# Memory sets between layer 1's gathers, its rows zero-filled in two halves within the layer, and some of layer 0's routing asked for later

## The chip, the cores and the metric

The kernel runs on one core of a Trainium2 chip. The core has a tensor engine (TensorE, PE in the profile) with its weight loads (PEld), a vector engine (VectorE, DVE), a scalar engine (ScalarE, ACT), GpSimd (POOL), and SyncE (SP), which here only issues DMAs. The metric is device time in microseconds (us) of one execution; the number that counts is the median of several.

## What is computed

Two transformer layers in float32, over 8 batches of 256 tokens with 128 channels. Each layer is an attention and a mixture of experts (MoE), each behind a layer norm whose scale and shift come from a conditioning vector. In short:

```
h = layernorm(x) * (1 + ca) + sa
x = x + ga * attention0(h)        # causal, 16 heads of 8, with biases
h = layernorm(x) * (1 + cb) + sb
x = x + gb * ffn0(h)              # shared gelu expert 128-512-128
                                  # + the best 2 of 8 such experts, softmax gates
h = layernorm(x) * (1 + ca) + sa
x = x + ga * attention1(h)        # causal, 16 heads of 64, no biases
h = layernorm(x) * (1 + cb) + sb
x = x + gb * ffn1(h)              # h + shared SwiGLU expert 128-64-128
                                  # + the best 2 of 16 such experts, sigmoid gates
```

The modulation vectors `sa` to `gb` are different for the two layers.

## The kernel before

**Stages.** The order of all instructions on each engine is the order in which the Python program asks for them; there is no scheduler. Layer 0's attention is a loop of 24 units, three for a batch, and layer 1's one of 32 units, four for a batch. A unit asks for its scores (PE), their exponentials (ACT, L1136 and L1673), the causal selects (POOL, L822) and, in the next unit, the product with the values (`o`, L1154 and L1692). Other work is hung on the units by number: `at(n, ...)` asks for it ahead of a unit's values, `at_end(n, ...)` behind everything of that unit, and `at_head(n, head, ...)` behind the causal select of one of its heads.

**Routing.** Tokens are sorted to experts in DRAM. For a span of batches the router's logits give each token's two best experts (a dozen small DVE operations, L850 to L857), PE counts how many earlier tokens chose the same expert (`rk`, L917 to L920), DVE turns that into a row number (`at`, `pick`, `slot`, `idx`, L922 to L928), and POOL writes the tokens to their rows by indirect DMAs, called scatters (L932). Each of these pieces is one step of a generator, so that they can be asked for apart: a step is one `go()`. The rows of layer 0 are `xs` of object `z0` (8.4 MB), those of layer 1 `xs` of object `z1` (24,576 rows of 128 floats, 12.6 MB). Both are zeroed first, since rows that no token takes are read too: `clear` (L888) issues one DMA on SP's queue that writes a zero tile over and over. Both fills are issued in set-up, one behind the other, and the loads of layer 0's expert weights (`wst`, L1495) come after them on the same queue. The first scatter of each layer waits for its fill.

**Layer 0's MoE** runs all its tokens in 39 tiles of 128 rows through the experts, beside the start of layer 1. The gates of its shared path: `gates0` (L1249 on) takes the difference of the two best logits on DVE, a tanh on ACT (L1252), and two more operations on DVE; `turn_gates0(w)` (L1284 on) transposes them on PE (`gp`, L1285) and copies them to SBUF (`gT`, L1288), on ACT for the first two windows of 512 tokens. Layer 0's routing hangs on the units in spans of batches (0,1), (2,3), (4), (5), with the first two spans' ranks asked for with `at(n + 4, go)`.

**Layer 1's MoE.** Batches 0 to 5 are sorted, scattered and run in 10 groups of 4 tiles (`turn1`, `hidden1`, `project_tiles`), and POOL fetches the results back for each token with 24 indirect DMAs, called gathers: `gather1(j)` for j = 0 to 11, two each (L1058). Batches 6 and 7 are not sorted: they go through all 16 experts, weighted by the gates: `dense_hidden(p)` for p = 0 to 7 computes two experts' gate and up products on PE (`gud`, L1942), a SiLU on ACT and a product on DVE (`a`, L1936 and L1937); `dense_gate` multiplies by the gates (L1947) and `dense_project` projects (`of`, L1952). `combine1` adds the gathered rows, weighted, on PE (`of`, L2018).

**The end of the program.** Behind the last group's projection the program asks for the 24 gathers; then for gates, `weigh1` (the diagonal matrices `dg`, L2010, on ACT), the shared expert and `dense_hidden(0)`; `gate_rows(1)` (the transpose `gT`, L1917, copied by DVE in L1919); `dense_hidden(1)` and `(2)`; the second step of `flag()`; `dense_hidden(3)`, and so on to `dense_hidden(7)` with combines and projections between. The products `gud`, `gT` and `good_cnt` share one PSUM tag of two buffers, taken in turn, so each waits until the one before the last has been read. `flag()` sets `bad`, which decides whether a general fallback has to run; it does not in the runs here:

```
yield
cnt = pp.tile([1, 1], F32, tag="s", name="good_cnt")
nc.tensor.matmul(out=cnt, lhsT=whole, rhs=nums[:, 1:2], start=True, stop=True)
nc.vector.tensor_scalar(bad, cnt, most[0:1, :], 1.0, ALU.is_lt, ALU.mult)
```

`most` is a tile of one column that holds a constant. Layer 0 has a helper that writes this constant again with POOL, `apart_on_gpsimd()` (L1404 and L1405), and `scatter(go, times)` calls it ahead of each of layer 0's scatters.

**The last batch of layer 1's attention** is normalised by `spread_last(us)` for two units at a time: PE spreads the reciprocals (`rp`, L1733) and DVE multiplies (L1737); `finish1(B - 1)` then projects it (`y`, L1745).

Of the kernel before, what the change touches and what calls it, by code (L numbers as in the profile page):

```python
# [9 lines left out]
F32 = mybir.dt.float32  # L10
# [6 lines left out]
P = 128  # L17
# [15 lines left out]
WAIT = mybir.DependencyInfo(mybir.DependencyClass.Sync, mybir.DependencyReason.DATA)  # L33
# [524 lines left out]
def fast_path(ctx: ExitStack, tc: tile.TileContext, i: dict, out: bass.AP, bad: bass.AP):  # L558
# [3 lines left out]
    nc = tc.nc  # L562
# [60 lines left out]
    for base, cm, step in ((0, 1, -D0), (D0 - 1, -1, D0)):  # L623
        nc.gpsimd.affine_select(
            out=hm, in_=hm, compare_op=ALU.is_ge, fill=0.0, base=base,
# [93 lines left out]
    def spread(t, rd, first, n):  # L719

        nc.sync.dma_start(
            out=t.rearrange("p k b c -> p (k b c)"),
            in_=rd[first : first + n].rearrange("k b c -> (k b c)").partition_broadcast(P),
        )
# [136 lines left out]
    class Sorted:  # L861


        def __init__(self, pool, tag, ne, nt, nd):
            self.pool, self.tag, self.ne, self.nt, self.nd = pool, tag, ne, nt, nd
            self.cap = cap = nt * P
            self.placed = 0
            f32 = lambda shape, name: pool.tile(shape, F32, name=f"{name}{tag}")
            self.s12 = f32([P, nt, 2, ne], "s12")
            self.slot = f32([P, nt, 2], "slot")  # L870
            self.region = f32([P, ne], "region")

            self.seen = pool.tile([P, nt + 1, ne], BF16, name=f"seen{tag}")
            self.yidx = pool.tile([P, nt, 2], I32, name=f"yidx{tag}")
            self.rowi = pool.tile([P, nd], I32, name=f"rowi{tag}")
            self.widx = pool.tile([P, nd], I32, name=f"widx{tag}")
            self.xs = dram.tile([ne * cap, P], F32, name=f"xs{tag}")
            self.ys = dram.tile([(ne + nd) * P, P], F32, name=f"ys{tag}")
            nc.gpsimd.tensor_scalar(self.region, num[:, :ne], float(cap), 0.0, ALU.mult, ALU.add)
            nc.gpsimd.memset(self.seen[:, 0, :], 0.0)  # L880
            self.marks = [pool.tile([P, 7, ne], BF16, name=f"marks{tag}{n}") for n in range(E1 // ne)]
            for t in self.marks:
                nc.gpsimd.memset(t[:, 0:3, :], 0.0)
# [1 line left out]
        def tmp(self, shape, name, dt=F32, bufs=2):  # L885
            return self.pool.tile(shape, dt, tag=name, bufs=bufs, name=f"{name}{self.tag}_{self.n}")

        def clear(self, zero):  # L888
            m = zero.shape[1]
            self.fill = nc.sync.dma_start(  # L890
                out=self.xs.rearrange("(p a) c -> p (a c)", p=P).rearrange("p (n m) -> p n m", m=m),
                in_=zero.unsqueeze(1).to_broadcast([P, self.ne * self.cap // m, m]),
            ).ins
            self.scatters = []

        def place(self, *args):
            for _ in self.place_steps(*args):
# [39 lines left out]
        def apart(self, ins):  # L937


            group = f"scatters{self.tag}"  # L940
            if self.scatters:
                tc.declare_no_dep(ins, group=group, reason="different rows")
                tc.add_manual_dep(ins, self.fill.name, WAIT, reason="rows are cleared first")
            tc.add_to_no_dep_group(group, ins)
            self.scatters.append(ins)

# [105 lines left out]
                in_offset=bass.IndirectOffsetOnAxis(ap=self.widx[:, d : d + 1], axis=0),  # L1052
            )

        def gather(self, yg, j):

            for k in range(2):
                nc.gpsimd.indirect_dma_start(  # L1058
                    out=yg[:, k, :], out_offset=None, in_=self.ys[:, :],
                    in_offset=bass.IndirectOffsetOnAxis(ap=self.yidx[:, j, k : k + 1], axis=0),  # L1060
                )
# [13 lines left out]
    SPANS0 = ((0, 2), (2, 2), (4, 1), (5, 1), (6, 1), (7, 1))  # L1075
# [169 lines left out]
    def gates0(first, nt):  # L1245

        ts = bass.ds(first, nt)
        g = g12[:, ts]
        name = f"g0_{first}"  # L1249
        th = ap0.tile([P, nt, 1], F32, tag="red", name=f"th{name}")  # L1250
        nc.vector.tensor_tensor(th, g[:, :, 0:1], g[:, :, 1:2], ALU.subtract)
        nc.scalar.activation(th, th, AF.Tanh, scale=0.5)  # L1252
        yield
        nc.vector.tensor_scalar(g[:, :, 0:1], th, 0.5, 0.5, ALU.mult, ALU.add)
        nc.vector.tensor_scalar(g[:, :, 1:2], th, -0.5, 0.5, ALU.mult, ALU.add)
        pick = ap0.tile([P, nt, 2, E0], F32, tag="pickg", bufs=1, name=f"pick{name}")
        nc.vector.tensor_tensor(pick, z0.s12[:, ts], g.unsqueeze(3).to_broadcast([P, nt, 2, E0]), ALU.mult)
        nc.vector.tensor_tensor(gates[:, ts, 0:E0], pick[:, :, 0, :], pick[:, :, 1, :], ALU.add)
# [24 lines left out]
    def turn_gates0(w):  # L1283
        gp = ps_ln([P, P], f"gp0_{w}")  # L1284
        nc.tensor.transpose(gp, gates[:, bass.ts(w, TT), :].rearrange("p j e -> p (j e)"), ident)  # L1285
        gT = hid0["g", w] = ap0.tile([P, P], F32, tag="gT", bufs=2, name=f"gT0_{w}")
        if w < 2:
            nc.scalar.copy(gT, gp)  # L1288
        else:
            nc.vector.tensor_copy(gT, gp)  # L1290

    def shared_project0(w):
        for _ in shared_project_steps0(w):
# [97 lines left out]
    def at(n, *steps):  # L1391
        early.setdefault(n, []).extend(steps)

    def at_end(n, *steps):
        ends.setdefault(n, []).extend(steps)
# [28 lines left out]
    for w in range(1, NW):  # L1424
        measure, normalise, modulate = layernorm_parts(w, md[0], SA, CA, f"0a{w}", ps_ln)
        n = 6 * w - 6
# [6 lines left out]
    ways = {}  # L1433
# [9 lines left out]
    for bs in SPANS0[:4]:  # L1443
        n = 3 * sum(bs) + 2
        measure, normalise, modulate, tokens = norms0[bs]
        go = ways[bs] = one(route0(bs))
        at_end(n, measure)
        at(n + 2, modulate)
        if bs[1] > 1:
            at(n + 2, tokens)  # L1450
        at_end(n + 2, go)
        if bs[1] == 1:
            at_end(n + 2, tokens)
        if bs[0] < 5:
            at(n + 3, go)
        if bs[0] < 4:
            at(n + 4, go)
        elif bs[0] == 4:
            at_end(n + 4, go)
        for unit, head in spots[bs[0]]:  # L1460
            at_head(unit, head, lambda go=go: scatter(go, 1))
    first_gates, last_gates = one(gates0(0, 8)), one(gates0(8, 8))
    at_end(17, first_gates)
    at_end(20, first_gates)
    norm6, norm7 = norm0(SPANS0[4]), norm0(SPANS0[5])
    at_end(23, norm6[0], lambda: turn_gates0(0), lambda: turn_gates0(1), lambda: ways[SPANS0[3]]())

    project0(0)
    project_v0(0)
# [3 lines left out]
    zero = ap0.tile([P, 512], F32, tag="hst", bufs=3, name="zero")  # L1473
# [8 lines left out]
    def set_up():  # L1482
        rd0 = rows_of(0, md[0])
        spread(mdb0, rd0, GA, 4)
        spread(gb0.unsqueeze(1), rd0, GB, 1)
        w1.update({n: load(w1p, n, nc.sync) for n in ("wo1", "gate_w", "wg1", "wu1", "wd1")})
        for n in range(2):
            nc.sync.dma_start(out=wds1[bass.ts(n, I1), :], in_=i["wds1"])
        nc.sync.dma_start(out=gate_b, in_=i["gate_b"].partition_broadcast(P))
        nc.sync.dma_start(out=bp32, in_=i["bp32"])  # L1490
        z0.clear(zero)
        z1.clear(zero)
        for e in range(E0 - 3):
            wst.append(ap0.tile([P, WPK], F32, tag=f"wst{e}", bufs=1, name=f"wst{e}"))
            nc.sync.dma_start(out=wst[e], in_=i["wpk"][bass.ts(e, P), :])  # L1495
        nc.gpsimd.memset(gates, 0.0)
        nc.gpsimd.memset(gates[:, :, E0 : E0 + 1], 1.0)
# [56 lines left out]
    scatter(go7, 4)  # L1554
    hides[1]()
    hides[1]()
    last_gates()
    one(shared_add0(0))()
    hides[1]()
# [437 lines left out]
    sums, diags = {}, {}  # L1997

    def gather1(j):
        k, n = divmod(j, 3)  # L2000
        if n == 0:
            sums["yg", k] = lp.tile([P, 3, 2, P], F32, tag="pt", bufs=4, name=f"yg1_{k}")
        z1.gather(sums["yg", k][:, n], j)

    def weigh1(w):

# [30 lines left out]
        return layernorm_parts(w, md[1], SA, CA, f"1a{w}", ps_ln)  # L2037

    spread(mdb1, rd1[0], GB, 4)
    nc.vector.memset(on, 0.0)  # L2040
    for n in range(4):
        nc.vector.memset(on[:, n, bass.ts(n, 8)], 1.0)
# [56 lines left out]
    for n in range(N):  # L2099
        b, u = divmod(n, 4)  # L2100
        scores1(b, u, behind.pop(n, {}))
        if n == 0:
            nc.gpsimd.memset(sel, 0.0)
            nc.gpsimd.affine_select(
                out=sel, in_=sel, compare_op=ALU.not_equal, fill=1.0, base=0,
                pattern=[[-8, 4], [-32, 2], [-64, 2], [0, D1]], channel_multiplier=1,
            )
        if n + 2 < N:
            project_qk1(*divmod(n + 2, 4))
        for step in early.pop(n, ()):  # L2110
            step()
        if n:
            values1(*divmod(n - 1, 4))
        if n + 2 < N:
            project_v1(*divmod(n + 2, 4))
        if u == 0 and b:
            reciprocals1(b - 1)
        for step in ends.pop(n, ()):
            step()

# [21 lines left out]
    norms[0][0]()  # L2142
    project_tiles(2)
    hidden1(4)
    spread_last((0, 1))
    turn1(5)
    norms[0][1]()
    project_tiles(3)
    norms[0][2]()
    spread_last((2, 3))  # L2150
    turn1(6)
    project_tiles(4)
    hidden1(5)
    go6()
    finish1(B - 1)
# [173 lines left out]
```

## Time and profile before

| | us |
|---|---|
| median of 14 runs | 604.07 |
| fastest and slowest of them | 598.14, 608.71 |
| the profiled execution | 607.14 |
| its span | 605.3 |

| engine | busy us | share of the span |
|---|---|---|
| PE | 542.7 | 90% |
| PEld (weight loads, beside PE) | 385.4 | 64% |
| DVE | 322.4 | 53% |
| POOL | 270.6 | 45% |
| ACT | 263.3 | 43% |

The page gives busy time per engine, then the span in 40 slices of about 15.1 us (a digit is the busy share in tenths, and in the row PEclk the clock that the throttle granted PE), the DMA queues, the chain of work that ended last, and the costliest groups of instructions. In a timeline line the numbers are start and duration; the brackets hold the idle time of the engine before the instruction and what ended it; "remote" there is a releaser that the profile doesn't show, "issue" is time in which the engine waited for nothing that it shows. The mean granted clock of the profiled execution was 0.959 of full speed. The 24 gathers of layer 1's end belong to the group of 56 at L1058, mean 962 ns each; the memory sets of layer 0 (L1405, 128x1) are 32, mean 112 ns. The fills move 20.5 MB of the 85.4 MB that all DMAs move.

### The profile page before, as it was taken

The numbers are of one execution on the slowest core, as the hardware profiler recorded it, in microseconds if no ns is written. First come the engines' busy times: TensorE is split into PE (matmuls) and PEld (weight loads), VectorE is DVE, ScalarE is ACT, GpSimd is POOL, SyncE is SP. The second block draws the span as 40 slices with busy tenths as digits, with TensorE's granted clock in tenths as the row PEclk, the third lists the DMA queues.
The fourth block names the chain that finished last, engine by engine and source line by source line (L and its number), as shares of the span: only waits on it lengthen the run. The fifth ranks groups of instructions, "written<-read, shape, count | busy, mean of one in ns | idle before, by whom it ended". The sixth has DMA issues, their size and how long they took to land.

```text
span 605.3 us, 11998 instructions
## 1 busy us (share of the span) xinstructions
PE 542.7 (90%) x4499; PEld 385.4 (64%) x4499; DVE 322.4 (53%) x986; ACT 263.3 (43%) x494; POOL 270.6 (45%) x400
## 2 busy tenths in 40 slices
PE   5999988899999998999999999999989898960594
PEld 4355544467999996666767676767667576830264
DVE  5258784675422224654456646556474957660154
ACT  3678764344566632763344423452625421250010
POOL 5224575664444214756223545340654530787300
PEclk9999997899999999999999999999999998996688
DMA  8699994234999813104030312103030366551401
GB/s 272 243 400 406 395 352 183 66 106 127 313 344 347 281 36 129 63 22 93 5 71 11 69 34 73 30 3 71 19 87 15 85 196 171 158 138 54 98 19 56
DMA packets 53566, 85.40 MB, mean 141 GB/s; under 512 B 6652, under 2 KB 32764, under 8 KB 52348
## 3 DMA queue, kind: packets, MB, share of 16 engines
q1 hardware_dynamic: 45308, 60.50, 31.5%
q0 software_dynamic: 8048, 23.67, 11.9%
q8 instruction: 37, 0.61, 0.4%
q10 hardware_dynamic: 144, 0.39, 0.2%
q14 instruction: 29, 0.24, 0.1%
HBM read 53.46 MB, written 31.07 MB: 140 GB/s over the span
## 4 chain that ended last, share of the span: by engine, by line
PE 74%; DVE 12%; another core or an unknown queue 6%; ACT 4%; issue 2%; DMA 1%; POOL 0%; DVEq 0%; ACTq 0%; POOLq 0%
PE sc L1670 7%; PE o L1692 6%; PE hp L1353 6%; PE yt L1361 6%; PE qp L1639 5%; PE y L1745 5%; PE sc L1120 5%; PE vp L1652 4%; PE kp L1639 4%; PE sum L1700 3%; PE o L1154 3%; PE gud L1942 2%; PE hp L1273 2%; PE qk L1084 2%; PE ysh L1302 2%
## 5 line engine op out<-in xcount | busy, mean ns | idle before, releaser
L822 POOL TENSOR_SCALAR_AFFINE_SELECT pt<-pt 128x256 f32<-128x256 f32 (+1 forms) x144 | 68.1, 500 | 154.2 <-ACT pt L1673 115.6
L1058 POOL DMA_INDIRECT yg<-ys,yidx x56 | 53.9, 962 | 38.3 <-DMA ys<-ysb 19.9
L1673 ACT ACTIVATE pt<-sc 128x768 f32<-128x768 f32 x64 | 48.4, 808 | 26.1 <-PE sc L1670 26.0
L1136 ACT ACTIVATE pt<-sc 128x1024 f32<-128x1024 f32 x48 | 46.6, 1027 | 20.1 <-PE sc L1120 15.5
L1670 PEld LDWEIGHTS sc<-q,k 64*128 64x128 f32 x512 | 41.5, 187 | 18.9 <-issue 13.9
L1670 PE MATMUL sc<-q,k 64*128 64x256 f32 (+1 forms) x512 | 50.5, 336 | 0.0
L1692 PE MATMUL o<-pt,v 128*64 128x256 f32 (+1 forms) x512 | 49.0, 332 | 1.7 <-DVE ou L1704 1.7
L1355 ACT ACTIVATE hst<-hp,wt 128x128 f32<-128x128 f32 x136 | 38.9, 369 | 25.7 <-ACT hst L1355 24.6
L1655 ACT COPY v<-vp 128x512 f32<-128x512 f32 x32 | 18.8, 586 | 67.1 <-PE vp L1652 67.1
L1050 POOL DMA_INDIRECT wt<-in_wpk_dram,widx x31 | 29.6, 953 | 33.9 <-PE xT L1344 29.8
L1692 PEld LDWEIGHTS o<-pt,v 128*64 128x64 f32 x512 | 32.0, 136 | 18.9 <-POOL pt L822 5.7
L1643 DVE COPY q<-qp 128x512 f32<-128x512 f32 x32 | 22.0, 688 | 35.9 <-PE qp L1639 35.9
L1639 PE MATMUL qp<-h,wq 128*128 128x256 f32 x128 | 36.1, 404 | 3.3 <-DVE q L1643 2.0
L1366 DVE COPY ysb<-yt 128x128 f32<-128x128 f32 x39 | 11.4, 292 | 50.0 <-PE yt L1361 50.0
L1120 PE MATMUL sc<-qm,k 32*128 32x512 f32 x192 | 35.8, 723 | 2.3 <-ACT pt L1136 1.7
L932 POOL DMA_INDIRECT xs<-ht0b,idx x32 | 32.1, 1002 | 12.0 <-issue 11.4
L1652 PE MATMUL vp<-wv,h 128*128 128x512 f32 x64 | 36.0, 645 | 0.0
L1353 PE MATMUL hp<-xTs,wt 128*128 128x128 f32 x272 | 35.9, 275 | 0.0
L1361 PE MATMUL yt<-wt,hst 128*128 128x128 f32 x272 | 35.8, 275 | 0.0
L1353 PEld LDWEIGHTS hp<-xTs,wt 128*128 128x128 f32 x272 | 33.0, 192 | 0.0
L1361 PEld LDWEIGHTS yt<-wt,hst 128*128 128x128 f32 x272 | 33.0, 192 | 0.0
L1639 PE MATMUL kp<-h,wk 128*128 128x256 f32 x128 | 32.9, 380 | 0.0
(306 smaller groups left out, 1078.6 us busy)
## 6 DMA issues: line engine op xcount, KB each, us to landing
xs<-zero SPq DMA_DIRECT2D x1, 12288.0 KB
xs<-zero SPq DMA_DIRECT2D x1, 8192.0 KB
rb<-rd SPq DMA_DIRECT2D x14, 512.0 KB
mdb<-mrd SPq DMA_DIRECT2D x2, 2048.0 KB
xg<-xs SPq DMA_DIRECT2D x63, 64.0 KB
wt<-in_wpk_dram SPq DMA_DIRECT2D x24, 128.0 KB
wst<-in_wpk_dram SPq DMA_DIRECT2D x5, 514.0 KB
ys<-ysb SPq DMA_DIRECT2D x10, 256.0 KB
```

Of the source, the lines that this page charges most:

```text
L822: nc.gpsimd.affine_select(out=pt, in_=pt, compare_op=ALU.is_ge, fill=0.0, base=0, pattern=[[0, pt.shape[1]], [1, P]], channel_multiplier=-1,)
L1058: nc.gpsimd.indirect_dma_start(out=yg[:, k, :], out_offset=None, in_=self.ys[:, :], in_offset=bass.IndirectOffsetOnAxis(ap=self.yidx[:, j, ...
L1120: nc.tensor.matmul(out=sc[:, n, :].rearrange("p (a q) -> p a q", q=rhs.shape[2]), lhsT=k[r, cols], rhs=rhs, start=True, stop=u < 2,)
L1136: nc.scalar.activation(pt[:, bass.ts(half, 2), :], sc, AF.Exp)
L1353: nc.tensor.matmul(out=hp[:, c, :], lhsT=wt[:, bass.ts(c, P)], rhs=xT, start=True, stop=True)
L1355: nc.scalar.activation(hs[:, c, :], hp[:, c, :], AF.Gelu_apprx_tanh, bias=wt[:, WB + c : WB + c + 1])
L1361: nc.tensor.matmul(out=y, lhsT=hs[:, c, :], rhs=wt[:, bass.ds(WF + c * P, P)], start=(c == 0), stop=(c == FC - 1))
L1639: nc.tensor.matmul(out=ps_[:, n, :], lhsT=w1[f"w{what}1"][:, bass.ts(2 * u + n, P)], rhs=hb, start=True, stop=True)
L1652: nc.tensor.matmul(out=vp, lhsT=hb[:, bass.ts(j, P)], rhs=w1["wv1"][:, bass.ts(half, 512)], start=True, stop=True)
L1670: nc.tensor.matmul(out=sc[:, n, cols], lhsT=k[r, m, bass.ts(kb, P)], rhs=q[r, m, qs], start=True, stop=True)
L1673: nc.scalar.activation(pt, sc[:, :, 0:384], AF.Exp, scale=1.0 / math.sqrt(D1))
L1692: nc.tensor.matmul(out=o[bass.ts(n, D1), m, qs], lhsT=v[:, kb, bass.ts(4 * (u % 2) + 2 * m + n, D1)], rhs=pts[m][:, n, cols], start=(kb == ...
```

## The change

1. `gather` takes a function that it calls before each of its two indirect DMAs, and `gather1` passes `apart_on_gpsimd`. So POOL writes `most` ahead of each of the 24 gathers, and `bad`, which reads `most`, comes behind the last of these writes.
2. The zero-fill of layer 1's rows leaves set-up. A new tile `zero1` (128x512) is set by POOL at the start of layer 1, ahead of that layer's first gather of layer 0's results, and the fill is issued in two halves of 6.3 MB on SP's queue, behind `reciprocals1(1)` at the end of unit 8 and behind `reciprocals1(2)` at the end of unit 12. Layer 1's first scatter, in unit 15, waits for both halves.
3. In layer 0, the ranks of the first two spans are asked for behind unit n + 4 rather than ahead of its values, and the step of batch 4 that was ahead of the values of unit n + 3 is now behind that unit. The generator `gates0` has one more stop: the subtraction on DVE is asked for at the end of unit 17, the tanh at the end of unit 18, the rest at the end of unit 20. The gates of window 0 are transposed at the end of unit 21, those of window 1 at the end of unit 22, both formerly at the end of unit 23, and DVE makes the copy `gT` for all windows.
4. `spread_last((0, 1))` moves behind `project_tiles(3)` and `spread_last((2, 3))` behind `project_tiles(4)`.

```diff
-        def clear(self, zero):
+        def clear(self, zero, part=0, parts=1):
             m = zero.shape[1]
-            self.fill = nc.sync.dma_start(
-                out=self.xs.rearrange("(p a) c -> p (a c)", p=P).rearrange("p (n m) -> p n m", m=m),
-                in_=zero.unsqueeze(1).to_broadcast([P, self.ne * self.cap // m, m]),
-            ).ins
-            self.scatters = []
+            n = self.ne * self.cap // m // parts
+            rows = self.xs.rearrange("(p a) c -> p (a c)", p=P).rearrange("p (n m) -> p n m", m=m)
+            self.fills.append(
+                nc.sync.dma_start(
+                    out=rows[:, bass.ts(part, n), :], in_=zero.unsqueeze(1).to_broadcast([P, n, m])
+                ).ins
+            )
...
-                tc.add_manual_dep(ins, self.fill.name, WAIT, reason="rows are cleared first")
+                for fill in self.fills:
+                    tc.add_manual_dep(ins, fill.name, WAIT, reason="rows are cleared first")
...
-        def gather(self, yg, j):
+        def gather(self, yg, j, between=lambda: None):
 
             for k in range(2):
+                between()
                 nc.gpsimd.indirect_dma_start(
...
         nc.vector.tensor_tensor(th, g[:, :, 0:1], g[:, :, 1:2], ALU.subtract)
+        yield
         nc.scalar.activation(th, th, AF.Tanh, scale=0.5)
...
-        if w < 2:
-            nc.scalar.copy(gT, gp)
-        else:
-            nc.vector.tensor_copy(gT, gp)
+        nc.vector.tensor_copy(gT, gp)
...
-        if bs[0] < 5:
+        if bs[0] < 4:
             at(n + 3, go)
-        if bs[0] < 4:
-            at(n + 4, go)
+            at_end(n + 4, go)
         elif bs[0] == 4:
+            at_end(n + 3, go)
             at_end(n + 4, go)
...
     at_end(17, first_gates)
+    at_end(18, first_gates)
     at_end(20, first_gates)
     norm6, norm7 = norm0(SPANS0[4]), norm0(SPANS0[5])
-    at_end(23, norm6[0], lambda: turn_gates0(0), lambda: turn_gates0(1), lambda: ways[SPANS0[3]]())
+    at_end(21, lambda: turn_gates0(0))
+    at_end(22, lambda: turn_gates0(1))
+    at_end(23, norm6[0], lambda: ways[SPANS0[3]]())
...
-        z1.clear(zero)
...
-        z1.gather(sums["yg", k][:, n], j)
+        z1.gather(sums["yg", k][:, n], j, apart_on_gpsimd)
...
     spread(mdb1, rd1[0], GB, 4)
+    zero1 = lp.tile([P, 512], F32, bufs=1, name="zero1")
+    nc.gpsimd.memset(zero1, 0.0)
...
             reciprocals1(b - 1)
+            if b in (2, 3):
+                z1.clear(zero1, b - 2, 2)
...
     hidden1(4)
-    spread_last((0, 1))
     turn1(5)
     norms[0][1]()
     project_tiles(3)
+    spread_last((0, 1))
     norms[0][2]()
-    spread_last((2, 3))
     turn1(6)
     project_tiles(4)
+    spread_last((2, 3))
```

More of the change, by code (lines that the diff above doesn't have):

```diff
@@ L867, in __init__ @@
             self.placed = 0
+            self.fills, self.scatters = [], []
             f32 = lambda shape, name: pool.tile(shape, F32, name=f"{name}{tag}")
@@ L1556, in fast_path @@
     hides[1]()
+    last_gates()
     last_gates()
```

## The prediction

> **What bounds the kernel now.** I read the page's 40 slices first, then the chain of waits at the end, the waits and the timeline around it, and last the windows.
>
> ```profile
> PE   5999988899999998999999999999989898960594
> PEclk9999997899999999999999999999999998996688
> ```
>
> TensorE (PE) is busy nine tenths nearly everywhere, so a microsecond off another engine is worth something only where PE stands. That is in slices 6 to 8 (75 to 121 us, layer 0's late attention) and above all in slices 36 and 37 (545 to 575 us). The granted clock falls in the same places.
>
> ```profile
> 537.14 2.43 ACT dg L2010 x8
> 539.58 19.38 another core or an unknown queue
> 558.98 0.60 ACT a L1936
> 559.58 11.42 another core or an unknown queue
> 571.02 0.61 ACT a L1936
> ...
> 572.99 8.39 PE gud L1942 x12
> ...
> ACT a L1936 <- remote: 30.9, 2, 19.4
> PE gud L1942 <- issue: 16.4, 1, 16.4
> ```
>
> The chain has 30.8 us put down to nobody, and the waits give the same to two activations of `a` (30.9 us in 2). The timeline tells whom they await:
>
> ```profile
> 544.37 0.95 POOL L1058 DMA_INDIRECT yg<-ys,yidx  x1 [0.30 <-issue]
> ...
> 542.74 1.02 PE L1942 MATMUL gud<-h,wu 128*128 128x512 f32 x2
> 543.60 0.38 PE L1917 MATMUL gT<-ident,gates 128*16 128x128 f32 x2
> 558.98 0.60 ACT L1936 ACTIVATE a<-gud 128x512 f32<-128x512 f32 x1 [19.41 <-remote]
> 559.61 0.69 DVE L1937 TENSOR_TENSOR a<-a,gud 128x512 f32<-128x512 f32 x1 [16.78 <-issue]
> 560.36 2.07 PE L1942 MATMUL gud<-h,wg 128*128 128x512 f32 x2 [16.37 <-issue]
> 571.02 1.08 ACT L1936 ACTIVATE a<-gud 128x512 f32<-128x512 f32 x2 [11.44 <-remote]
> 572.86 0.20 DVE L2030 TENSOR_SCALAR bad<-good_cnt,most 1x1 int32<-1x1 f32 x1
> ```
>
> The first `gud` ends on PE at 543.76, but ScalarE (ACT) learns of it at 558.96: 15.2 us. `gT` ends at 543.98 and VectorE (DVE) copies it at 562.50; the third `gud`, ending at 566.5, reaches ACT at 571.0. Hand-overs that do not start at PE are prompt in the same stretch: ACT to DVE 0.03 us (559.58 to 559.61), DVE to PE 0.06 (560.30 to 560.36). Throughout it GpSimd (POOL) issues 24 gathers back to back, 536.74 to 567.5, each 0.95 after 0.30. So PE's reports come late while POOL runs gathers. The windows give PE's loss:
>
> ```profile
> 542.00:560.00 18.00, 1.98 (x6) 0.64 (x5) 1.19 (x3) 0.60 (x1) 13.73 (x15) 0.67 0.29 72
> 566.50:573.00 6.50, 0.21 (x4) 0.09 (x3) 1.35 (x3) 1.08 (x2) 0.07 (x1) 0.67 0.83 170
> 573.00:580.00 7.00, 7.00 (x10) 2.96 (x11) 1.34 (x3) 0.90 (x2) 0.00 (x0) 0.57 0.02 5
> ```
>
> (Columns: window, its length, busy time and instructions of PE, weight load, DVE, ACT, POOL, then clock, DMA share, GB/s.) After 573.0 PE never stops until 596.44.
>
> **The change, part by part**, against the profiled execution's 607.14 us (span 605.3 and 1.8 around it); the median, 604.07, lies 3.07 lower, and I take the same difference off at the end.
>
> *Memsets between the gathers.* Layer 0's scatters already run so: starts 94.56, 95.83, 97.09, 98.36, a period of 1.265 against 1.25 for the gathers; the memset (0.12) fills the pause. 24 x 0.015 = 0.36 us, on POOL only. What they do to the late reports is not seen for gathers. Nearest rows, layer 0's runs with memsets: in a run of five (92.96 to 99.32) an end at 95.45 reached ACT at 100.43, with reports let through at 97.55 and 98.98 between; in a run of four (112.2 to 117.25) the lags were 1.1 and 1.7; in a run of eight, 0.9 at most. Layer 1's early runs of four gathers without memsets (from 224.29 and 237.51) show no lag either, so these rows do not settle it; only the run of 24 shows 15 us. Bounds: 1 us per hand-over, or the unchanged lag; I take up to 5, being a run with memsets. Then gud1, gud2 and gud3, three hand-overs behind 543.8, are done by about 561. What is late next: `bad` (L2030) reads `most`, and the build makes it wait for POOL's last memset, after 23 gathers: 537.0 + 23 x 1.265 - 0.2 = 565.9. Behind `bad` on DVE stand all later products, and gud4 needs its PSUM buffer: it starts about 566.3.
>
> From gud4's start to 596.44 PE's work was 2.6 us at half clock (576.42 to 579.0, worth 1.29) and 17.44 at full: 18.73. The clock was half in stretches of whole multiples of 3.41 us (507.3 to 510.7, 548.3 to 565.4, 568.8 to 579.0), so on one grid of windows, and came back after the first fully busy one: 568.8 to 572.2 here. Work done 566.3 to 572.2 at half: 2.95; the other 15.78 ends at 588.0. Gain 8.4. Without any half clock it would be 11.4; with nothing let through 0. Of the gathers' data the last is wanted by the `of` of L2018 at 596.26, 8 us earlier now, 588; the DMA engines were busy with them until 573.
>
> The Trainium skill ("TensorE: Matmul & The Clock Gate", What's actually happening) has a free-running window of 3.41 us, one idle window halving the clock and one busy one restoring it; the trace's grid agrees, but recovery took 5.0 us after 560.36 and 6.0 after 572.99. Counting 3.41 us from PE's restart would end the half clock at 569.7, for 1.2 us more gain, which I leave out.
>
> *Layer 0's order.* Three gaps before PE are named by the lines moved:
>
> ```profile
> 86.52 0.18 PE L917 MATMUL rk<-marks,before 128*128 128x32 bf16 x1 [0.90 <-DVE mall L913]
> ...
> 88.68 2.04 PE L1120 MATMUL sc<-qm,k 32*128 32x512 f32 x8 [0.89 <-ACT pt L1136]
> ...
> 117.09 0.33 PE L1285 MATMUL gp<-ident,gates 128*128 128x128 f32 x1 [2.06 <-ACT gT L1288]
> ```
>
> Ranks asked for after the values' matmuls (o, 1.07 us at 86.73) cover the 0.90. The scores at 88.68 wait for exps that stood behind the tanh (87.51, itself 3.71 late on DVE): put behind them it frees 0.89. The two gT copies, a unit apart and on DVE, take 2.05. Sum 3.8. Each was followed by a half-clock stretch of 3.4 us with PE busy (90.9 to 94.3, 118.2 to 121.6), worth 1.7 each: 7.2 at most. The 2.22 before `y` at 98.6 (ACT's late `ht0b`) stays. Lower end 0: later ranks make picks, indices and scatters later, and DVE (8.54 of 10.9 us busy there) has two copies more, 0.54. I take 4.5.
>
> *The fill.* 12.58 MB leave layer 0's queue, 31 us at its 400 GB/s (slices 3 and 4); the expert weights behind it (issued until 86.9) land earlier, but PE waited for none: 0. In layer 1 each half is 6.29 MB, 15.7 us, issued after the `rb` loads, at 309.3 and 344.25. SP has nothing else until 341.3 and 371.8. The new tile's memset costs what `zero`'s did, 0.53 us, in front of POOL's gather at 237.51, which followed 3.77 us idle: 0. The first scatter now waits for both halves:
>
> ```profile
> 360.11 1.01 POOL L932 DMA_INDIRECT xs<-ht,idx  x1 [0.28 <-issue]
> 361.15 0.77 POOL L822 TENSOR_SCALAR_AFFINE_SELECT pt<-pt 128x256 f32<-128x256 f32 x2
> ```
>
> With the 79 GB/s already moving there (1.34 MB in 17 us) the second half ends at 344.25 + 7.63/0.400 = 363.3, 3.2 us late for the scatter. Behind it are the causal selects that PE's values want at 367.4; they end at 361.9, so 5.5 us cover it; at the slowest rate with a fill running (352 GB/s, slice 6) it is 5.8 late. Cost 0.5, bounds 0 and 3. Past 365.6, where the cover ends, each microsecond counts once.
>
> The skill's rule against this ("DMA: Bandwidth & Descriptors", Specifications) is a limit of about 358 GB/s per core; the trace's 395 to 406 GB/s for this very fill is more, so the measurement decides; by the rule the half would land at 365.6, at the very end of the cover, and the sum would stay.
>
> *The last batch's spread.* `rp` (L1733) stood 1.50 and 0.67 us for DVE's `aq`, then ran 507.3 to 510.7 at half clock. A tile later it follows filled work: 2.2 of idle, 1.7 of clock, less if the stall goes to the next `aq`; `y` (515.89) could wait instead. Bounds 0 and 3; I take 1.3.
>
> Sum: -8.4 + 0.4 - 4.5 + 0.5 - 1.3 = **-13.3**, 593.8 on the profiled execution, **590.8** on the median.
>
> **Rivals.**
> 1. *The memsets let nothing through.* Reports still come at about 559 and 571. For it: 24 without pause is the only place with 15 us, so length alone may do it; runs of four with and without memsets hardly differ. Against: reports at 97.55, 98.98 and 100.41 inside a run with memsets. Only layer 0 and the spread gain: 0.4 - 4.5 + 0.5 - 1.3 = -4.9, **599.2**.
> 2. *The memset itself holds PE's reports until the run ends.* For it: short gather runs without it show no lag, short runs with it do. gud0 would be read at 571.0 and gud3 start at 580.6 (two half-clock `gud` of 3.43, hand-overs of 1.4), 7.6 late; 3 of it comes back from full clock: +4.6, **603.8** with the other terms -4.9.
> 3. *The fill arrives late (the slower side).* One scatter holds POOL, the selects behind it, PE's values. Price: one for one beyond 365.6. It eats the 13.8 us gained elsewhere when the fill ends after 379.4, that is below 7.63/35.2 = 217 GB/s; 3.5 us more, 197 GB/s, makes **607.6**. For it: while layer 0's 2 KB fill packets ran, everything else on SP stood 38 us behind; the `xs` rows share a queue order with it. Against: 350 GB/s or more in every slice it had.
>
> **How the numbers follow.** Forecast 0.52, rival 1 0.19, rival 2 0.12, rival 3 0.17. Predicted 590.8. The low end adds the far bounds, 3.0 of clock and half of the 4.4 left in layer 0 and spread, 2.2: 585.6, so 585; the high end takes in rivals 1 and 2: 604. No change means within 0.5%, 601.1 to 607.1, about what can be told here. Faster: forecast 0.50, rival 1 0.14, rival 2 0.03 = 0.67. Same: 0.02 + 0.05 + 0.06 + 0.02 = 0.15. Slower: the rest, 0.18, nearly all rival 3.
>
> **What would show it.** Right: ACT's `a` waits under 6 us each, `bad` released by POOL near 566 and PE running on from there at half clock for one or two windows; no gaps at 85.6, 87.8 and 115.0; the scatter near 360 held 2 to 4 us with no gap on PE. Wrong: 15 us waits still there (rival 1), all reports after the last gather (2), or selects waiting on a fill (3).

## The result, and the profile after

| | before | changed |
|---|---|---|
| median, us | 603.74 (47 runs) | 610.39 (10 runs) |
| lowest to highest | 596.76 to 608.71 | 608.33 to 613.21 |
| ratio | | 1.0141 (1.0110 to 1.0171) |
| profiled execution, its span | 607.14, 605.3 | 611.11, 609.4 |

The changed kernel is slower, by 6.65 us between the medians. Medians, here and below, are over all executions and ratios over those within 1.5% of their kernel's fastest, so that a ratio is not the quotient of two medians (here that would be 1.0110). Some line numbers differ from those of the kernel before: the gathers are L1063, the sets L1408, `a` L1942 and L1943, `gud` L1948, `bad` L2036, `rk` L920, `gp` L1291, `rp` L1739.

PE's row and the granted clock in the page's 40 slices:

```profile
PE   5999997799999999999999999999989898860394
PEclk9999998999999999999999998999999998995598
```

As in the profile before, PE has one deep hole near the end (slices 36 and 37, counted from 0, now a 0 and a 3). Slices 6 and 7 (91 to 122 us) have 7 where they had 8. A hole of 2 us about 365 us is too small for this row and has to be looked for in the timeline.

The chain of waits in the end (start, length, what), then the waits (engine, line, what was waited for: us in total, times, longest):

```profile
539.14 2.43 ACT dg L2016 x8
541.58 30.30 another core or an unknown queue
571.87 0.59 ACT a L1942
...
573.23 5.42 PE gud L1948 x8
...
DVE a L1943 <- ACT a L1942: 40.4, 8, 28.8
PEld gud L1948 <- DVE a L1943: 30.6, 3, 28.7
ACT a L1942 <- remote: 30.3, 1, 30.3
PE gud L1948 <- DVE a L1943: 29.7, 2, 28.4
```

The two waits put down to nobody, 19.38 and 11.42 us, have become one of 30.30. The timeline of the same stretch (start, duration, engine, line, operation; in brackets the idle time before it and its end):

```profile
544.43 0.38 PE L1923 MATMUL gT<-ident,gates 128*16 128x128 f32 x2
...
566.19 0.12 POOL L1408 MEMSET most<- 128x1 f32 x1
566.50 0.94 POOL L1063 DMA_INDIRECT yg<-ys,yidx  x1 [0.19 <-issue]
...
571.85 0.60 ACT L1942 ACTIVATE a<-gud 128x512 f32<-128x512 f32 x1 [30.28 <-remote]
572.48 0.69 DVE L1943 TENSOR_TENSOR a<-a,gud 128x512 f32<-128x512 f32 x1 [28.78 <-ACT a L1942]
573.09 0.41 DVE L1925 COPY gTs<-gT 16x256 f32<-16x256 f32 x1
...
579.91 0.20 DVE L2036 TENSOR_SCALAR bad<-good_cnt,most 1x1 int32<-1x1 f32 x1
```

PE's first `gud` ended at 544.59 and was read 27.3 us later, 4.4 us after the last gather was over; `gT`'s copy came with it. `bad` stands behind `good_cnt` (578.76) and not behind the last set (566.3): in this execution its new wait cost nothing. The windows show the hole in numbers (length, then busy time and instructions of PE, PEld, DVE, ACT, POOL, clock, DMA share, GB/s):

```profile
545.00:571.90 26.90, 0.00 (x0) 0.00 (x0) 0.00 (x0) 0.05 (x1) 19.00 (x36) 0.58 0.17 48
571.90:580.00 8.10, 5.53 (x10) 2.17 (x10) 2.39 (x5) 1.75 (x3) 0.00 (x0) 0.70 0.42 102
580.00:590.00 10.00, 9.96 (x43) 6.09 (x44) 5.64 (x10) 2.39 (x4) 0.00 (x0) 1.00 0.17 41
```

Where layer 1's scatter begins, SP's queue, POOL and PE:

```profile
341.30 0.58 SPq L894 DMA_DIRECT2D xs<-zero  x1
...
365.52 1.01 POOL L935 DMA_INDIRECT xs<-ht,idx  x1 [8.75 <-DMA xs<-zero]
366.55 0.77 POOL L822 TENSOR_SCALAR_AFFINE_SELECT pt<-pt 128x256 f32<-128x256 f32 x2
367.02 1.22 PE L1698 MATMUL o<-pt,v 128*64 128x256 f32 x8 [1.91 <-POOL pt L822]
```

The scatter waits 8.75 us for the second half of the fill, and PE waits 1.91 us for the selects behind it.

Setting each of PE's instructions against the same one of the profile before gives how far it runs ahead (-) or behind (+): -3.2 us at 185 us (behind layer 0's attention), -3.1 at 356, **+1.0** at 381 (behind the held scatter), +0.5 at 485, +0.9 at 518 (behind the spread), +0.8 at gud0, **+4.1** from 581 on. So between these two executions layer 0 gained 3.2, the fill lost 4.1, the spread lost 0.4 and the tail (from gud0 on) lost 3.2.

### The profile page after: what moved, and what is told of

The parts are those of the page before. It is cut to its first block, busy times and chain, and to the rows that moved or that the text cites. A ratio compares the mean times of both kernels' runs of the same rounds, so it can differ in the third digit from the quotient of the medians.

```text
span 609.4 us, 12026 instructions
## 1 busy us (share of the span) xinstructions
PE 538.0 (88%) x4499; PEld 383.3 (63%) x4499; DVE 324.4 (53%) x988; ACT 262.7 (43%) x492; POOL 272.2 (45%) x425
## 3 DMA queue, kind: packets, MB, share of 16 engines
q0 software_dynamic: 8048, 23.67, 11.8%
## 4 chain that ended last, share of the span: by engine, by line
PE 69%; DVE 12%; another core or an unknown queue 5%; DMA 5%; ACT 4%; issue 3%; POOL 1%; SPq 0%; DVEq 0%; POOLq 0%; ACTq 0%
PE sc L1676 6%; PE hp L1356 6%; PE yt L1364 6%; PE o L1698 5%; PE sc L1125 5%; PE qp L1645 5%; PE y L1751 4%; PE vp L1658 4%; DMA xs<-zero 4%; PE kp L1645 4%; PE sum L1706 3%; PE o L1159 3%; PE gud L1948 2%; PE qk L1089 1%
## 5 line engine op out<-in xcount | busy, mean ns | idle before, releaser
L1063 POOL DMA_INDIRECT yg<-ys,yidx x56 | 53.7, 958 | 32.4 <-DMA ys<-ysb 20.2
L1948 PE MATMUL gud<-h,wg 128*128 128x512 f32 x16 | 9.4, 674 | 29.7 <-DVE a L1943 29.7
```

The lines of the kernel that those rows point to most:

```text
L1063: nc.gpsimd.indirect_dma_start(out=yg[:, k, :], out_offset=None, in_=self.ys[:, :], in_offset=bass.IndirectOffsetOnAxis(ap=self.yidx[:, j, ...
```

## The experiments

Kernels sent together ran on one chip and share the runs of the kernel before. Several chips were drawn, and they turned out to be of two kinds: on the first, the kernel before takes 601 to 604 us (so also where the result was measured), on the second 573. All ratios are against before on the same chip.

**One part at a time, first kind** (before 602.52).

e1_memsets: only these lines.

```diff
-        def gather(self, yg, j):
+        def gather(self, yg, j, between=lambda: None):
...
             for k in range(2):
+                between()
                 nc.gpsimd.indirect_dma_start(
...
-        z1.gather(sums["yg", k][:, n], j)
+        z1.gather(sums["yg", k][:, n], j, apart_on_gpsimd)
```

> The kernel before with only the memory sets between the 24 gathers. Theory A (the sets, or the run of gathers with them, keep PE's reports back until the run is over): gud0 is read by ACT about 4 us after the last gather, as in the changed kernel (571.9 there), and the time is 3 to 5 us above before's median, with little scatter. Theory B (the sets change nothing; the changed kernel's profiled execution was one draw of a lottery that before plays as well): a report is let through in the middle of the run as in before (559), and the time is within 1.5 us of before.

Measured: 604.73, ratio 1.0012 (0.9966 to 1.0058). gud0 was read 22.5 us late, 1.4 us after the last gather. The place in the trace is nearer to theory A. The time lies between the two: 0.7 us over before by the ratio, which is theory B's, 2.2 by the medians, and the interval of the ratio reaches into both theories.

e2_fill: the zero tile, the two halves and the wait for both, as in the change, and nothing else.

> The kernel before with only the zero-fill moved into layer 1 in two halves. Theory A: the first scatter waits for the second half as in the changed kernel (a gap of about 2 us before PE's o at 367 and one half-clock window behind it), so 3.5 to 4.5 us slower. Theory B (the fill cost something in layer 0 as well, hidden so far): less than 2 us slower. The changed kernel's PE was 0.7 us ahead from 29 us on, which the fill's move may have done: 3.3 rather than 4.

Measured: 603.44, 1.0007 (0.9962 to 1.0051). In its profile the scatter waits 8.3 us for the fill, and PE falls back by 2.1 us there, not 4; the time is in theory B's range.

e3_layer0: the edits of `gates0`, `turn_gates0` and the hooks alone.

> The kernel before with only layer 0's edits (ranks, tanh, batch 4, turned gates, gT on DVE). Theory A: PE is 2.5 to 3.2 us ahead from 125 us on, and the time 2.5 to 3.2 us lower. Theory B: what is gained there is lost in the end, since POOL's gathers are released by the last tiles alone and the late report's time sets the end: within 1 us of before.

Measured: 601.98, 1.0031 (0.9988 to 1.0074). PE was 2.6 us ahead of the first profile at 185 us, as theory A has it, but the time is theory B's (the median is 0.5 us lower). A reason came from the other runs of this group: with layer 0's order untouched PE was 6.6 (e1), 6.3 (e2) and 3.3 us (e4) ahead of that first profile at the same place. The first profile was of an execution 3.4 us above its kernel's median, and against it alone a gain of 3 us can't be shown.

e4_pauses: the 24 gathers in groups of four.

```diff
-    for j in range(TT * LAST):
-        gather1(j)
+    def gathers(*js, after=None):
+        if after is not None:
+            nc.gpsimd.tensor_copy(seen[:, 0, 0, after : after + 1], hid[after][:, 0:1])
+        for j in js:
+            gather1(j)
+    gathers(0, 1)
...
     dense_hidden(0)
+    gathers(2, 3, after=0)
```

and so on: 4, 5 after 2; 6, 7 after 4; 8, 9 after 5; 10, 11 after 6.

> The kernel before with the 24 gathers asked for in six groups of four, each group after the first behind a tiny POOL copy that reads the product a of dense_hidden(0), (2), (4), (5), (6), so that POOL stands still until PE's reports have come through. Theory A (a run of gathers keeps PE's reports back, a pause lets them through): no ACT wait above 6 us in the tail, end 5 to 12 us earlier than before. Theory B (the reports are late for another reason, such as PE itself waiting): gud0 is still read 10 us or more late, POOL waits with it, and the end is 5 to 20 us later than before.

Measured: **590.20, 0.9795** (0.9735 to 0.9856), from four executions. ACT's activations in its tail:

```profile
543.34 0.60 ACT L1936 ACTIVATE a<-gud 128x512 f32<-128x512 f32 x1 [3.07 <-PE gud L1942]
546.74 0.60 ACT L1936 ACTIVATE a<-gud 128x512 f32<-128x512 f32 x1 [2.79 <-PE gud L1942]
...
565.82 0.60 ACT L1936 ACTIVATE a<-gud 128x512 f32<-128x512 f32 x1 [9.94 <-remote]
```

gud0 (PE's end 543.31) is read at once, and so are the five products behind it; the last two are read 7.1 and 7.9 us late (PE's end 558.7 and 562.3). From gud0's start to PE's end it is 38.9 us; in before 55.5. So an unbroken run of gathers goes with the held reports, and breaking it up releases most of them. Whether it is POOL's standing still that does it isn't shown: only the second and the last group had a pause before them (3.6 and 1.6 us). The groups two to five ran from 545.07 to 565.61 with 0.35 to 0.76 us between them, and the five reports of `gud` up to 555.28 still came at once.

**One part less, second kind** (before 572.62; a chip on which nothing had been expected to differ).

> The changed kernel without the sets between the gathers (fill, layer 0's edits and the spread's move stay). Alone, the sets cost 0.1% (0.5 either way), the fill 0.1%, layer 0's edits 0.3%; together all parts cost 1.4%. Theory A (the sets keep the reports back to the end of the run): some report comes through inside the run of gathers, the tail from gud0 to the end is 60 to 64 us instead of 66.8, and the time is 604 to 606. Theory B (the sets change nothing, the rest makes up the 1.4%): 608 or more.

> The changed kernel with the zero-fill back in set-up. Theory A (the held scatter costs 4 us of PE and clock in layer 1): 605 to 607, about 4 below the changed kernel. Theory B (the fill's move is made good elsewhere, as its run alone at 1.0007 of before suggests): 609 or more.

> The changed kernel with layer 0 as before (sets, fill and the spread's move stay). Theory A (the edits gain nothing: with layer 0 as before PE was 0, 3.3, 6.3 and 6.7 us ahead of the first profile by 125 us in four profiled executions, with the edits 2.5 and 3.2): 606 to 610, at or below the changed kernel. Theory B (they gain 3 us): 613 or more.

| the changed kernel without | median | ratio | gud0 to PE's end |
|---|---|---|---|
| the sets (e5) | 572.73 | 0.9995 (0.9970 to 1.0019) | 29.9 us |
| the fill (e6) | 587.95 | 1.0269 (1.0243 to 1.0295) | 45.9 us |
| layer 0's edits (e7) | 589.50 | 1.0303 (1.0277 to 1.0329) | 45.2 us |

On this chip every `gud` of the profiled executions is read 0.04 us after PE's end, during the gathers too. None of the times expected was met, since they were written for the first kind; the ratios say that here the loss, 15 to 17 us, goes with the sets and with nothing else.

e8_private puts 24 sets into before in the same places, each on a column that nobody else touches (the call is left out here):

```diff
+    def apart_quietly():
+        n = sums["turn"] = sums.get("turn", -1) + 1
+        nc.gpsimd.memset(sums["quiet"][:, 0, 0, n : n + 1], 0.5)
```

> The kernel before with 24 sets between the gathers, each on a column of its own of a tile that nothing else touches, so that nobody waits for them and they signal nobody. Theory C (what keeps PE's report back is that the sets on one column each report too, and take the few moments in which a report gets through): a report of PE's comes through inside the run as in before, tail 60 to 64 us. Theory A (any GpSimd work between the gathers, or the longer run, does it): as with the sets on one column, first report about 4 us after the last gather, tail 65 us or more.

Measured: 570.99, 0.9983 (0.9962 to 1.0004), tail 29.9 us. As no report is held on this chip, it tells nothing of theory C; it does say that 24 sets cost nothing by being there.

**The whole and its variants side by side, second kind** (before 573.09).

> The changed kernel itself, beside its own parts on one chip. So far two kinds of chip were met: on one the kernel before takes 603 us and PE's reports are held back during the run of gathers; on the other it takes 572.6 and they are not, there the sets alone made +15 us, because bad waits on DVE for the last set and all later products stand behind it. Theory D (both hold: a chip of the first kind hides that wait behind the held reports): 610 or +1.0 to 1.7% on a chip of the first kind, 588 or +2.7 to 3.1% on one of the second. Theory E (the sets' cost is the same everywhere, 15 us, and the first chip's +1.4% had gains of some 8 us beside it): +1.4% on both.

> The changed kernel without the sets, on the same chip as the whole. Theory D: 1.0007 or so of before on either kind of chip (0.9995 was seen on the second kind); on the first kind 3 to 6 us below the whole, on the second 15. Theory E: 15 us below the whole on both.

> The changed kernel with each set on a column of its own of a tile that nobody reads: the sets stay in POOL's queue, nobody waits for them and they report to nobody. Theory D: the same as without sets, within 0.4%, on either chip. A theory by which a set holds up the gathers or PE's reports by being there: as the whole.

| | median | ratio |
|---|---|---|
| the changed kernel (e9) | 588.63 | 1.0268 (1.0239 to 1.0296) |
| without sets (e10) | 572.75 | 0.9985 (0.9954 to 1.0017) |
| sets on private columns (e11) | 573.26 | 1.0010 (0.9985 to 1.0036) |

On this kind of chip theory D holds and E falls: 15.9 us between e9 and e10, and the private sets give nearly all of it back. The waits and the timeline of e9 show by which wait:

```profile
DVE bad L2036 <- POOL most L1408: 15.2, 1, 15.2
PE gud L1948 <- DVE bad L2036: 13.4, 1, 13.4
...
533.71 1.02 PE L1948 MATMUL gud<-h,wu 128*128 128x512 f32 x2
534.76 0.60 ACT L1942 ACTIVATE a<-gud 128x512 f32<-128x512 f32 x1 [2.62 <-PE gud L1948]
...
539.77 0.19 PE L2035 MATMUL good_cnt<-nums,whole 128*1 128x1 f32 x2
...
556.23 0.12 POOL L1408 MEMSET most<- 128x1 f32 x1
556.38 0.20 DVE L2036 TENSOR_SCALAR bad<-good_cnt,most 1x1 int32<-1x1 f32 x1 [15.19 <-POOL most L1408]
556.52 0.67 DVE L1943 TENSOR_TENSOR a<-a,gud 128x512 f32<-128x512 f32 x1
...
556.64 2.07 PE L1948 MATMUL gud<-h,wg 128*128 128x512 f32 x2 [13.41 <-DVE bad L2036]
```

gud0 ends at 534.73 and is read at 534.76. `good_cnt` was ready at about 540, and `bad` runs 0.03 us after the last set's end. DVE works in program order, so all later products stand behind it, and the next `gud` needs the PSUM buffer of `good_cnt`; PE restarts at half the clock (2.07 us for two matmuls, which took 1.12 at full clock).

e12_pauses_again is e4's kernel.

> The kernel before with the gathers in six groups of four with pauses, as measured before at 0.9795. On a chip of the first kind again 0.975 to 0.985. On one of the second, where nothing is held back, the pauses only put the last gathers later (they ended at 572.9 rather than 567.5): 1.00 to 1.02.

Measured: 574.23, 1.0009 (0.9985 to 1.0034): no gain where nothing is held, and no loss.

**The whole again, first kind** (before 601.18).

> The changed kernel again, for a chip of the first kind (before 603 us): 1.010 to 1.017 of before. On one of the second kind (before 573): 1.024 to 1.030, as seen.

> The changed kernel without sets. Theory D (the sets are the whole of the loss, by the wait of bad and, on a chip of the first kind, by reporting while reports are held): 0.995 to 1.003 of before on either kind. Theory F (on a chip of the first kind the late fill and layer 0's order cost it): 1.008 or more there.

> The changed kernel with sets on private columns that nobody waits for. If the wait of bad is what costs: as without sets, on either kind. If a set's presence between gathers holds PE's reports on a chip of the first kind: as the whole there (1.010 to 1.017).

| | median | ratio | gud0 read after its end by |
|---|---|---|---|
| the changed kernel (e13) | 604.92 | 1.0102 (1.0048 to 1.0156) | 11.8 us |
| without sets (e14) | 605.17 | 1.0076 (1.0043 to 1.0108) | 19.3 us |
| sets on private columns (e15) | 603.98 | 1.0061 (1.0016 to 1.0106) | 6.6 us |

The three intervals overlap, and without sets three quarters of the loss stay: on this kind of chip no part of it can be put down to the sets, and e14 lies at theory F's bound (1.008) rather than within D's (1.003). That a set holds reports back is not borne out: gud0 was read 27.3, 22.5 and 11.8 us late with sets on `most` (changed, e1, e13), 15.2, 11.5, 19.2 and 19.3 late without (before, e2, e3, e14), 6.6 with sets on private columns (e15). From gud0's start to PE's end it is 53.5 to 58.8 us with sets on `most`, 52.2 to 55.5 in the other five.

**What the rest costs**, written for a chip of the first kind and run on one of the second (before 572.56).

> Layer 0's edits and the spread's move alone. If the fill makes the rest of the loss on a chip of the first kind (before 603 us): 0.998 to 1.003 there; if these edits do: 1.005 or more. On a chip of the second kind (before 573): 0.994 to 1.000, since the fill's 1.2 to 1.6 us are gone.

> The fill's move and the spread's alone. If the fill makes the rest of the loss on a chip of the first kind: 1.004 to 1.009 there, with a gap of 1 to 2 us before PE's o about 367; if layer 0's edits do: 0.997 to 1.003. On a chip of the second kind: 1.001 to 1.004.

> The gathers in six groups of four, each group after the first behind a POOL copy that reads the product a of dense_hidden(0), (3), (5), (6), (7): in the first version the second and third groups ran together, and PE's reports were held from 551.8 to 556.6. On a chip of the first kind 0.970 to 0.980 (e4_pauses had 0.9795); on one of the second 1.00 to 1.01, since the last gathers come later.

Measured: e16 570.86, 0.9979 (0.9954 to 1.0004); e17 573.90, 1.0031 (1.0007 to 1.0055), with a gap of 0.94 us before `o`; both as expected for this kind. So here the fill with the spread costs 0.3%, and the layer 0 edits with the spread nothing that can be told. e18, the groups behind the products 0, 3, 5, 6 and 7, took 579.52, 1.0123 (1.0091 to 1.0155), more than expected. Its reason doesn't stand in e4's trace either: between 551.8 and 556.6 ACT read three products there, at 551.85, 553.56 and 555.28, each 0.04 us after PE's end. Here the last gather ended at 572.1 in a span of 581.5, and POOL waited for the products and PE for the gathered data:

```profile
POOL seen L2185 <- DVE a L1937: 8.5, 2, 5.0
...
PE of L2018 <- DMA yg<-ys,yidx: 5.1, 6, 1.4
```

## Why the prediction was wrong

**The tail, -8.4.** This term's mechanism failed, and with it the forecast. It rested on the sets letting PE's reports through in up to 5 us, a figure from runs of four to eight scatters. In the changed kernel the first came 27.3 us late, and over eight profiled executions on the first kind of chip, those with an unbroken run of gathers, the sets made no difference that shows. The tail lost 3.2 us instead of gaining 8.4. That is rival 2's picture, though not its reason: e13, with sets, had a report after 11.8 us, in the middle of the run. Why the reports are held stays open. A reading was off besides: the last gather of the profile before ended at 566.57 (565.63 + 0.94), not at 567.5, so the late report at 571.02 came 4.4 us behind the run there, as it does in the changed kernel.

**The wait of `bad`.** Place and time were right: the last set ended at 566.3 where 565.9 was worked out. What failed is the account it was put into. I set it against a `gud4` that the held reports delay to 576, so it looked like part of a gain. Had reports been prompt, `bad` would have run at about 550, an estimate (in e4 and e8, with prompt reports, it runs 6.4 us behind gud0's end), and the wait would be a new one of some 16 us; this is what the second kind of chip does (15.2 us on DVE, +2.7%). A rival with prompt reports and this wait was missing.

**The fill, +0.5.** Mechanism right, size wrong: 4.1 us in the profiled execution, 1.1 to 2.5 in the four others with it on the first kind, 1.2 to 1.6 on the second; no execution without the fill's move shifts there at all. I let the second half start at once and counted 19.1 us from its issue to its end. It took 24.2 (341.30 to the scatter at 365.52): until 347.0 the DMA engines moved only 221 GB/s, busy with the `rb` loads issued 1.1 us ahead of it on the same queue; from there to 364.0 it was 375, and the scatter followed 1.5 us later. Besides, PE was 3 us ahead and wanted its values at 365.1, not 367.4, so gains ahead of the scatter shortened the cover of 5.5 us. To the 1.91 us of idle came one stretch at half the clock, 368.5 to 371.9, worth 1.7.

**Layer 0, -4.5.** The gaps named at 85.6 and 87.8 are gone, but new ones stand where the moved steps went:

```profile
100.00 0.18 PE L920 MATMUL rk<-marks,before 128*128 128x16 bf16 x1 [0.99 <-DVE marks L912]
...
102.29 0.47 PE L1291 MATMUL gp<-ident,gates 128*128 128x128 f32 x1 [2.05 <-DVE vm L1106]
...
108.11 0.33 PE L1291 MATMUL gp<-ident,gates 128*128 128x128 f32 x1 [0.75 <-ACT ht0b L1221]
...
116.46 0.17 PE L920 MATMUL rk<-marks,before 128*128 128x16 bf16 x1 [1.73 <-DVE marks L912]
```

`gp` now waits 2.05 us for `vm`, as long as it waited for `gT` (2.06), and the ranks for `marks`. The larger fault was to take one execution for the kernel: at 185 us PE stood 0, 3.3, 6.3 and 6.6 us ahead of that profile with layer 0 as before, and 2.5 to 3.7 with the edits (five executions, first kind). So the edits gained nothing there that can be shown, and may have lost. On the second kind, together with the spread's move, they are within the noise (e16).

**The spread, -1.3.** It lost 0.4: PE waited 2.37 us before `yq_o` for DVE's `ysb`, then ran `rp` at half the clock (508.4 to 511.8).

```profile
507.47 0.48 PE L1899 MATMUL yq_o<-wd,aq 64*128 64x128 f32 x2 [2.37 <-DVE ysb L1905]
```

The stall went to the next product, the case that the prediction named ("less if the stall goes to the next `aq`") and didn't take. The size of this term isn't shown: over the same stretch the other three executions of the whole and its variants on the first kind shift by -0.9 to +1.8, four without the move by -1.2 to +0.6.

**The sum.** Between the two profiled executions it is -3.2 (layer 0) + 4.1 (fill) + 0.4 (spread) + 3.2 (tail) - 0.4 (small shifts in layer 1) = +4.1 us of span. The medians are 6.65 apart, for the profiled execution of before was 3.4 us above its median and that of the changed kernel 0.7. The highest case inside the range, rival 2 at 603.8, was 6.6 us short. On the profiled executions 4.4 of them are the fill (3.6), the spread (1.7) and layer 0 (1.3), less 1.4 at the tail and 0.8 of small terms. The rest is that 3.07 us were taken off because the profiled execution of before lay so far above the median of that time, while the changed kernel's lay only 0.7 above its own.

**What stays open.** On the first kind of chip the whole has 1.0141 and 1.0102, the whole without sets 1.0076, and each of the three parts that were run alone no loss that can be told (1.0012, 1.0007, 1.0031); the spread's move was never run alone. The one loss that each profiled execution with the part shows at its place is the fill's, 1.1 to 4.1 us, against some 4.6 us that the whole without sets loses by its ratio. How the loss divides between the fill, layer 0's order and the tail there wasn't settled: each of them also moves the moment at which the run of gathers or scatters meets PE's reports, and the delays of gud0 alone vary from 6.6 to 27.3 us.

## What to carry to other kernels

A write that is put into an engine's queue only to space out other work makes every reader of the written tile wait for the end of that queue: write to something that nobody reads (15.9 us here). Price a new wait against prompt reports as well as against the delay seen in one trace, since the delay may not be there on the next chip. A gap in one profile is a gain only if other executions of the same kernel have it too; and the cover of a late transfer shrinks by whatever the change gains ahead of it.

Of the kernels run, the one with paused gathers is best across both kinds of chip: 0.9795 of before on the first (four executions), 1.0009 on the second, where the changed kernel has 1.0102 to 1.0141 and 1.0268.

## What the runs showed of the hardware that was not expected

The same program takes 573 us on three of the chips drawn and 601 to 604 on the others. Most of the difference is visible at one place: gud0 is read 0.04 us after its end in all eleven profiled executions on those three, and 6.6 to 27.3 us after it in eight of nine on the others, the ninth being the one with pauses. From gud0's start to PE's end it is 29.9 to 32.0 us in seven executions on the former, those without sets on `most` and without e18's long pauses, and 52.2 to 58.8 in the eight. A smaller part lies in layer 0's late attention, where POOL issues the scatters: between 60 and 125 us PE gains 5.6 to 8.7 us on the first profile in the eleven, at most 5.7 in the others. The kernel before itself was profiled on the first kind alone. In order the delays of gud0 are 6.6, 11.5, 11.8, 15.2, 19.2, 19.3, 22.5 and 27.3 us; what sets them, and why a chip is of one kind or the other, no run here shows.
